# Softplus of delta for the other images in layer 0: three parts summed by TensorE, the positive part added by VectorE

## The chip, the cores and the metric

One NeuronCore of a Trainium2 chip runs the whole four-layer program as one launch. The time is the device time of one execution in microseconds (us); the number compared is the median of several executions. The other seven cores do nothing.

## The reference

Four layers act on an activation of 4 images x 64 x 64 tokens x 128 channels. Only layer 0, a selective scan (Mamba style) over 256 inner channels and 16 states, is touched. What matters of it:

```
xz = x @ w_in;  xc, z = split(xz)
xa = silu(depthwise_conv3x3(xc) + conv_b)              # 256 channels, 4096 tokens
dts, B, C = split(xa @ w_xproj, [8, 24])
delta = softplus(dts @ w_dt + b_dt)                    # 256 x 4096 for every image
# four directions (rows, columns, and both reversed) share delta, B and C:
h = h * exp(delta_i * A) + (delta_i * u_i) * B_i       # 16 states a channel, 4096 steps
y_i = sum_n h * C_i
```

The kernel computes softplus(x) as max(x, 0) + ln(1 + u) plus a small correction, with u = exp(-|x|): with w = 1 + u as rounded, the correction is u - (w - 1), that is, what the rounding of w lost.

## The kernel before

Layer 0 works image by image. For an image and a half h of the channels (128 of 256) there are 64 chunks of 64 tokens; the main loop runs over I, that is over 4 images x 2 halves x 64 chunks = 512 iterations. An iteration does, for the four directions in two pairs (kp = 0 and 1):

- `products(now, kp)` (L850): 16 small matmuls on TensorE that write delta*u*B of two directions into two PSUM buffers `db`. There are three such buffers.
- `scan(...)`: on VectorE, two adds of the carry into the first column (L865) and two scans of 1024 columns (L870), from `db` and the decay `dA` into the SBUF tile `big`; then on GpSimd the carry `cy` of the next chunk (L877) and the product of `big` with C (L885), 128 x 2048.
- `inputs(nxt)` (L826), VectorE, in the first half only: delta*u of the next iteration.
- `total(I - 2, part)` (L905): 8 matmuls on TensorE that sum the states of the iteration two back into the one PSUM tile `yp`; after part 1, ScalarE copies `yp` out in four pieces (L919). Part 0 of the next iteration writes `yp` again.
- `decay(w, ...)` (L773): on ScalarE, four exponentials for the next group of four chunks.

Beside this, a generator `beside` does the preparation of the next image in small steps. It is advanced once in the first half of an iteration (after `total(I - 2, 0)`, before the decays and `products(now, 1)`) and once in the second half (after `total(I - 2, 1)` and the four copies). All of its steps share one PSUM bank, `bg`. Images 1 to 3 go through `front` (norm and input projection) and then, from chunk 0 of the second channel half of the image before, through `middle`: eight blocks of 512 tokens, each of 14 steps, so seven iterations a block. Of a block's steps, numbered 0 to 13: 0 to 3 convolve and transpose, 4 projects, 5 turns B, 6 to 9 make delta for the two channel halves, 10 to 13 transpose and flip delta and store it. Even steps fall into first halves and odd ones into second halves. Image 0 is prepared before the loop by another function (`opening`), which the change leaves alone.

Steps 6 and 8 of before hold, for one half of the channels each, the matmul with `w_dt` (L426) and five ScalarE activations (L491 to L496): |x|, max(x, 0), u, w = 1 + u written into the bank, and ln w. Steps 7 and 9 hold the three VectorE operations L498, L501 and L502, which read and write the bank, and the store of delta (`keep_steps`, L432).

The loop stands under `tc.manual_schedule` for TensorE, ScalarE and VectorE: these three issue in exactly the order in which the program is written. GpSimd's and the DMA queue's (SP) order is the scheduler's. The SBUF tiles of the preparation come from a ring of ten buffers, `t2k`.

Of the kernel before, what the change touches and what calls it, by code (L numbers as in the profile page):

```python
# [8 lines left out]
AF = mybir.ActivationFunctionType  # L9
ALU = mybir.AluOpType  # L10
# [4 lines left out]
P = 128  # L15
# [5 lines left out]
BLK = 512  # L21
# [39 lines left out]
def tl(pool, shape, tag, dtype=F32, bufs=None):  # L61
    return pool.tile(shape, dtype, name=tag, tag=tag, bufs=bufs)
# [99 lines left out]
def layer0(cm, x, W, x1, also, ahead, kept):  # L162


    tc, nc = cm.tc, cm.nc
    wl = kept.enter_context(tc.tile_pool(name="l0k", bufs=1))
    dr = kept.enter_context(tc.tile_pool(name="l0dram", bufs=2, space=DRAM))
    with ExitStack() as ctx:
        ctx.enter_context(nc.allow_non_contiguous_dma(reason="parameters laid over partitions"))
        wp = ctx.enter_context(tc.tile_pool(name="l0w", bufs=1))  # L170
        tmp = ctx.enter_context(tc.tile_pool(name="l0t", bufs=10))
# [66 lines left out]
        for i in range(2):  # L238
            t = tl(wp, [P, QC, 2, NH0, TC], f"dA{i}")
# [16 lines left out]
        for i in range(2):  # L256
            t = tl(wp, [P, 8, PADW], f"padded{i}")
# [108 lines left out]
        def shifted(i, pool, tag, queue=nc.sync):  # L366

            k, h = divmod(i, 2)
            x3 = [tl(pool, [3 * CG, 2, 8 * PADW], tag) for _ in range(2)]
            for dy in range(3):  # L370
                s0 = (8 * k + dy) * PADW
                for i in range(2):
                    queue.dma_start(
                        x3[i][dy * CG : (dy + 1) * CG],
                        xc_d[4 * h + 2 * i : 4 * h + 2 * i + 2, :, s0 : s0 + 8 * PADW]
                        .rearrange("g p s -> p g s"),
                    )
            return x3

        def convolved(ps, h, x3):  # L380
            for dx in range(3):
                for g in range(4):
                    nc.tensor.matmul(  # L383
                        ps[g * CG : (g + 1) * CG, :], lhsT=cdiag[:, 4 * h + g, dx, :],
                        rhs=x3[g // 2][:, g % 2, :].rearrange(
                            "p (r w) -> p r w", w=PADW
                        )[:, :, dx : dx + HW],
                        start=(dx == 0), stop=(dx == 2),
                    )

        def columns(ps, src):
            for i in range(4):
                nc.tensor.transpose(
                    ps[:, i * P : (i + 1) * P], src[:, i * P : (i + 1) * P], cm.ident
                )

        def keep_turned(b, h, k, t):
            nc.sync.dma_start(
                img[b]["xT"][h, k * BLK : (k + 1) * BLK, :].rearrange("(t p) c -> p t c", p=P), t
            )  # L400

        def projected(ps, xa):
            for h in range(2):
                nc.tensor.matmul(
                    ps[0:NX, :], lhsT=w_xp[:, h, :], rhs=xa[h], start=(h == 0), stop=(h == 1)
                )

        def keep_c(b, k, xd):
            nc.sync.dma_start(
                img[b]["ct"][8 * k : 8 * k + 8].rearrange("c n t -> n c t"),  # L410
                xd[RANK + NST : NX, :].rearrange("n (c t) -> n c t", t=TC),
            )

        def turned_b(ps, k, xd, xr):
            pb = ps[:, 0 : 8 * NST].rearrange("p (c n) -> p c n", n=NST)
            for c in range(8):
                for j in range(2):
                    nc.tensor.matmul(
                        pb[j * TC : (j + 1) * TC, c, :],
                        lhsT=xr[0:NX, c, :] if j else xd[0:NX, c * TC : (c + 1) * TC],  # L420
                        rhs=cm.ident[0:NX, RANK : RANK + NST], start=True, stop=True,
                    )
            nc.vector.tensor_copy(BT[:, 8 * k : 8 * k + 8, :], pb)

        def steps(ps, h, xd):
            nc.tensor.matmul(  # L426
                ps, lhsT=w_dt[:, h * P : (h + 1) * P], rhs=xd[0:RANK, :],
                start=True, stop=True,
            )

        def keep_steps(b, h, k, r):
            nc.sync.dma_start(img[b]["dl"][h, :, k * BLK : (k + 1) * BLK], r)  # L432

        def flipped(ps, t):
            nc.tensor.matmul(
                ps, lhsT=flip, rhs=t.rearrange("p t c -> p (t c)"), start=True, stop=True
            )

        def keep_both(b, h, k, j, t):
            for i in range(2):  # L440
                nc.sync.dma_start(
                    img[b]["dT"][h, 8 * k + i : 8 * k + 8 : 2, j]
                    .rearrange("t r c -> r t c"), t[i * TC : (i + 1) * TC],
                )

        def middle(b, bank, pool, tag, ahead):

            ready = [shifted(i, pool, tag) for i in range(ahead)]
            for k in range(NBLK):
                cols = slice(k * BLK, (k + 1) * BLK)  # L450
                xa = []
                for h in range(2):
                    ps = bank()
                    convolved(ps, h, ready.pop(0))
                    if 2 * k + h + ahead < 2 * NBLK:
                        ready.append(shifted(2 * k + h + ahead, pool, tag))
                    xh = tl(tmp, [P, BLK], "t2k")
                    nc.scalar.activation(xh, ps, AF.Silu, bias=vec[:, 0, h : h + 1])
                    y0 = tl(tmp, [P, BLK], "t2k")
                    nc.scalar.activation(y0, xh, AF.Copy, scale=d4[:, h : h + 1])  # L460
                    nc.sync.dma_start(img[b]["y0"][:, h, cols], y0)
                    xa.append(xh)
                    yield
                    ps = bank()
                    columns(ps, xa[h])
                    t = tl(tmp, [P, 4, P], "t2k")
                    nc.scalar.copy(t, ps.rearrange("p (t c) -> p t c", c=P))
                    keep_turned(b, h, k, t)
                    yield
                ps = bank()  # L470
                projected(ps, xa)
                xd = tl(tmp, [P, BLK], "t2k")
                nc.scalar.copy(xd[0:NX, :], ps[0:NX, :])
                xr = tl(tmp, [P, 8, TC], "t2k")
                nc.scalar.copy(
                    xr[0:NX], ps[0:NX, :].rearrange("p (c t) -> p c t", t=TC)[:, :, ::-1]
                )
                keep_c(b, k, xd)
                yield
                turned_b(bank(), k, xd, xr)  # L480
                rs = []
                for h in range(2):
                    yield


                    ps = bank()
                    steps(ps, h, xd)
                    bias = vec[:, 1, h : h + 1]
                    u = tl(tmp, [P, BLK], "t2k")
                    r = tl(tmp, [P, BLK], "t2k")  # L490
                    nc.scalar.activation(u, ps, AF.Abs, bias=bias)  # L491
                    nc.scalar.activation(r, ps, AF.Relu, bias=bias)
                    nc.scalar.activation(u, u, AF.Exp, scale=-1.0)
                    nc.scalar.activation(ps, u, AF.Identity, bias=cm.ones[:, 0:1])
                    v = tl(tmp, [P, BLK], "t2k")
                    nc.scalar.activation(v, ps, AF.Ln)  # L496
                    yield
                    nc.vector.scalar_tensor_tensor(  # L498
                        ps, ps, 1.0, u, ALU.subtract, ALU.subtract
                    )  # L500
                    nc.vector.tensor_tensor(ps, v, ps, ALU.subtract)  # L501
                    nc.vector.tensor_tensor(r, ps, r, ALU.add)  # L502
                    keep_steps(b, h, k, r)
                    rs.append(r)

                yield
                for h in range(2):
                    t = None
                    for j in range(2):
                        ps = bank()  # L510
                        if j == 0:
                            columns(ps, rs[h])
                        else:
                            flipped(ps, t)
                        t = tl(tmp, [P, 4, P], "t2k")
                        nc.scalar.copy(t, ps.rearrange("p (t c) -> p t c", c=P))
                        keep_both(b, h, k, j, t)
                        yield
# [215 lines left out]
        def place(I):  # L734
            u, c = divmod(I, NCHUNK)
            return divmod(u, 2) + (c,)
# [237 lines left out]
        with tc.manual_schedule(engines=engines):  # L974
            for I in range(N):
                b, h, c = place(I)
# [19 lines left out]
                w = quads.get(I // QC + 1)  # L996
# [1829 lines left out]
```

## Time and profile before

| | |
|---|---|
| median of 3 executions | 10080.76 us (10066.63 to 10089.57) |
| the profiled execution | 10065.04 us, its span 10063.1 us |
| busy in the span | TensorE 8590.0, VectorE 7471.3, GpSimd 5373.5, ScalarE 5347.1 us |
| the chain that ended last | TensorE 42%, VectorE 26%, GpSimd 10% |
| the scans of layer 0 | from 219.5 us to 5653 us of the span |

The profile lists groups of equal instructions: line, engine, operation, output<-input with shapes and count, then total busy time in us and the mean of one in ns, then the idle time of that engine just before them and what ended most of it. The timeline lists instructions by start, with the duration; a bracket gives the idle time before and what ended it. Where equal instructions follow each other, the duration runs from the first start to the last end. A matmul's duration includes the way through the array, so the distance to the next start says more of the rate; a matmul of this type (f32) leaves two records. The table of stretches gives each engine's busy time and count in a stretch of the span, and the TensorE clock that was granted (1.00 is full speed).

### The profile page before, as it was taken

The page shows a single profiled execution, that of the slowest core. Times are in us where ns is not written, and L with a number is a line of the kernel's source. Part 1 is how long each engine was busy: PE and PEld are TensorE (multiplying, and loading weights), DVE is VectorE, ACT ScalarE, POOL GpSimd, SP SyncE. Part 2 cuts the span into 40 slices and gives each one's busy share as a digit, 9 for nine tenths or more (in the row PEclk, how much of TensorE's full clock was granted, in tenths as well). Part 3 has the DMA queues.
Part 4 walks back from the last instruction along what each step waited for, and adds up shares of the span by engine and source line. Part 5 has one row for each costly group of instructions (what it writes and reads, how often), then busy time and mean ns, then how long its engine had stood idle before and what let it go on. Part 6 is the DMA issues. An engine that isn't in the chain of part 4 may idle for free.

```text
span 10063.1 us, 193320 instructions
## 1 busy us (share of the span) xinstructions
PE 8590.0 (85%) x73048; PEld 4219.2 (42%) x73048; DVE 7471.3 (74%) x11089; ACT 5347.1 (53%) x13309; POOL 5373.5 (53%) x2788
## 2 busy tenths in 40 slices
PE   7888888889988899988888649999999958888776
PEld 3333444444434444444333334444444435554442
DVE  4999999999999999999999765454551123455656
ACT  5775555775547665556522237767776613443331
POOL 4999999899999899999999500000000000100000
PEclk8899999999999999999999869999999977888887
DMA  7344454445543455444333321111101062212101
GB/s 212 103 132 128 137 141 114 128 130 146 145 126 120 120 160 144 132 120 124 87 103 94 107 66 31 37 38 34 38 18 33 16 223 48 61 45 52 43 24 47
DMA packets 1081627, 957.38 MB, mean 95 GB/s; under 512 B 165356, under 2 KB 825616, under 8 KB 1073920
## 3 DMA queue, kind: packets, MB, share of 16 engines
q1 hardware_dynamic: 1055298, 880.82, 29.7%
q0 software_dynamic: 18560, 63.37, 3.4%
q8 instruction: 586, 9.60, 0.4%
q14 instruction: 337, 2.76, 0.1%
q10 hardware_dynamic: 6846, 0.83, 0.1%
HBM read 608.77 MB, written 335.80 MB: 94 GB/s over the span
## 4 chain that ended last, share of the span: by engine, by line
PE 42%; DVE 26%; POOL 10%; issue 8%; ACT 6%; DMA 5%; SPq 2%; DVEq 0%; ACTq 0%; POOLq 0%
DVE big L870 15%; POOL big L885 8%; PE qk L1758 7%; PE av L1817 7%; PE yp L905 5%; PE db L850 4%; PE x L2607 2%; DVE tex L2613 2%; DVE du L826 2%; PE s L2373 1%; DMA xo<-xT_d 1%; PE po L2398 1%; PE bg L383 1%; DVE mx L2337 1%; PE s L2331 1%
## 5 line engine op out<-in xcount | busy, mean ns | idle before, releaser
L885 POOL TENSOR_TENSOR big<-big,ct 128x2048 f32<-128x2048 f32 x1024 | 4659.0, 4550 | 76.1
L870 DVE TENSOR_TENSOR_SCAN big<-dA,db 128x1024 f32<-128x1024 f32 x2048 | 4571.0, 2273 | 13.6 <-DMA xo<-xT_d 8.6
L850 PE MATMUL db<-dg,du 32*64 32x256 f32 x32768 | 1896.0, 418 | 606.0 <-DVE big L870 466.6
L905 PE MATMUL yp<-big,both 128*64 128x256 f32 x16384 | 2229.3, 419 | 60.5 <-ACT yc L919 47.6
L905 PEld LDWEIGHTS yp<-big,both 128*64 128x64 f32 x16384 | 1191.8, 148 | 1031.0 <-issue 563.6
L850 PEld LDWEIGHTS db<-dg,du 32*64 32x64 f32 x32768 | 653.3, 135 | 1791.9 <-issue 1692.3
L1817 PE MATMUL av<-e,x 128*128 128x512 f32 x2048 | 974.0, 592 | 4.6 <-ACT e L1812 4.6
L1762 ACT ACTIVATE e<-qk,nk 128x512 f32<-128x512 f32 x1024 | 692.6, 685 | 534.1 <-PE qk L1758 533.2
L1758 PE MATMUL qk<-a,xT 128*128 128x512 f32 x2048 | 966.6, 594 | 8.6 <-ACT e L1762 7.9
L919 ACT COPY yr<-yp 128x64 f32<-128x64 f32 x1024 | 221.7, 216 | 1346.9 <-PE yp L905 1331.4
L818 ACT ACTIVATE dg<-mask,BT 128x32 f32<-128x32 f32 x4096 | 896.6, 318 | 10.9 <-PE db L850 8.6
L773 ACT ACTIVATE dA<-dp,A 128x252 f32<-128x252 f32 x2048 | 866.0, 498 | 49.8 <-issue 26.1
L1331 POOL TENSOR_TENSOR g_rs<-g_rs,k_qrow 128x4 f32<-128x4 f32 x32 | 41.0, 1282 | 1499.9 <-DVE g_rs L1330 1499.9
L1758 PEld LDWEIGHTS qk<-a,xT 128*128 128x128 f32 x2048 | 378.0, 190 | 462.3 <-issue 358.0
L1817 PEld LDWEIGHTS av<-e,x 128*128 128x128 f32 x2048 | 381.6, 190 | 434.7 <-issue 393.2
L1812 ACT ACTIVATE e<-e 128x1024 f32<-128x1024 f32 x510 | 538.7, 1056 | 15.4
L877 POOL TENSOR_TENSOR cy<-big,a 128x32 f32<-128x32 f32 x1008 | 365.6, 363 | 299.6 <-DVE big L870 239.3
L2380 ACT ACTIVATE e<-s 128x576 f32<-128x576 f32 x448 | 272.7, 647 | 398.8 <-PE s L2373 396.2
L2112 POOL TENSOR_TENSOR ln_rs<-ln_rs,mroot 128x4 f32<-128x4 f32 x64 | 64.8, 1012 | 756.0 <-DVE ln_rs L2111 501.6
L2392 POOL COPY vp<-vt 112x80 f32<-112x80 f32 x112 | 30.2, 270 | 781.2 <-PE po L2398 755.3
L2613 DVE SCALAR_TENSOR_TENSOR tex<-x,gw,tex 128x128 f32<-128x128 f32 x768 | 264.5, 344 | 198.0 <-PE x L2607 184.3
L826 DVE TENSOR_TENSOR du<-xo,dt 128x256 f32<-128x256 f32 x512 | 387.7, 757 | 0.0
(569 smaller groups left out, 9805.6 us busy)
## 6 DMA issues: line engine op xcount, KB each, us to landing
ct<-ct_d SPq DMA_DIRECT2D x1024, 128.0 KB
xo<-xT_d SPq DMA_DIRECT2D x2048, 32.0 KB
dg_d<-dg SPq DMA_DIRECT2D x256, 256.0 KB
dg<-dg_d SPq DMA_DIRECT2D x256, 256.0 KB
t4k<-xc_d SPq DMA_DIRECT2D x288, 132.0 KB
dp<-dl_d SPq DMA_DIRECT2D x256, 128.0 KB
dT_d<-t2k SPq DMA_DIRECT2D x256, 128.0 KB
dt<-dT_d SPq DMA_DIRECT2D x512, 64.0 KB
```

What stands on the lines that cost most here:

```text
L773: nc.scalar.activation(w["dA"][:, :, g, n, 1:], w["dp"][:, g, :, 1:], AF.Exp, scale=A[:, w["h"], g, n : n + 1],)
L818: nc.scalar.activation(q["dg"][:, n, :], mask, AF.Copy, scale=BT[:, q["c"], n : n + 1])
L826: nc.vector.tensor_tensor(q["du"], q["xo"], q["dt"].unsqueeze(1).to_broadcast([P, 2, P]), ALU.mult)
L850: nc.tensor.matmul(bs[j][p * TC : (p + 1) * TC, g * NH0 : (g + 1) * NH0, t0 : t0 + QR], lhsT=q["du"][rows, kp, g * TC : (g + 1) * TC], rhs ...
L870: nc.vector.tensor_tensor_scan(st[:, u].rearrange("p n t -> p (n t)"), q["w"]["dA"][:, c % QC].rearrange("p g n t -> p (g n t)"), bs[j].re ...
L885: nc.gpsimd.tensor_tensor(sv, sv, q["ct"].rearrange("p n t -> p (n t)").unsqueeze(1) .to_broadcast([P, 4, NH0 * TC]), ALU.mult,)
L905: nc.tensor.matmul(yp[p * TC : (p + 1) * TC], lhsT=both, rhs=st[:, :, p * NH0 + n, :], start=(n == 0), stop=(n == NH0 - 1),)
L1758: nc.tensor.matmul(ps, lhsT=me["xT"][:, kt * P : (kt + 1) * P], rhs=me["a"][k], start=True, stop=True,)
L1762: nc.scalar.activation(e[:, j, :], ps, AF.Exp, bias=me["nk"][:, kt : kt + 1], scale=2.0)
L1812: nc.scalar.activation(es[g + 2], es[g + 2], AF.Exp)
L1817: nc.tensor.matmul(avs[b, k], lhsT=img[b]["x"][:, kt, :], rhs=e[:, j, :], start=(kt == 0), stop=(kt == NT - 1),)
L2613: nc.vector.scalar_tensor_tensor(t[:, i, :], s[:, e * D : (e + 1) * D], gw[:, j, 4 * a + e : 4 * a + e + 1], t[:, i, :], ALU.mult, ALU.add,)
```

## The change

For both halves h, the ScalarE parts are now made first, in steps 6 and 7. w goes into an SBUF tile instead of the bank, and after ln w a sixth activation replaces w by 1 - w. Steps 8 and 9 then sum ln w, 1 - w and u by three matmuls with the identity into the bank, and one VectorE addition adds max(x, 0). The number of steps of a block stays 14. A block takes 20 tiles from the ring instead of 18.

```diff
                 turned_b(bank(), k, xd, xr)
+                parts = []
+                for h in range(2):
+                    yield
+                    ps = bank()
+                    steps(ps, h, xd)
+                    bias = vec[:, 1, h : h + 1]
+                    u, r, w, v = [tl(tmp, [P, BLK], "t2k") for _ in range(4)]
+                    nc.scalar.activation(u, ps, AF.Abs, bias=bias)
+                    nc.scalar.activation(r, ps, AF.Relu, bias=bias)
+                    nc.scalar.activation(u, u, AF.Exp, scale=-1.0)
+                    nc.scalar.activation(w, u, AF.Identity, bias=cm.ones[:, 0:1])
+                    nc.scalar.activation(v, w, AF.Ln)
+                    nc.scalar.activation(w, w, AF.Identity, scale=-1.0, bias=cm.ones[:, 0:1])
+                    parts.append([v, w, u, r])
                 rs = []
                 for h in range(2):
                     yield
                     ps = bank()
-                    steps(ps, h, xd)
-                    bias = vec[:, 1, h : h + 1]
-                    u = tl(tmp, [P, BLK], "t2k")
-                    r = tl(tmp, [P, BLK], "t2k")
-                    nc.scalar.activation(u, ps, AF.Abs, bias=bias)
-                    nc.scalar.activation(r, ps, AF.Relu, bias=bias)
-                    nc.scalar.activation(u, u, AF.Exp, scale=-1.0)
-                    nc.scalar.activation(ps, u, AF.Identity, bias=cm.ones[:, 0:1])
-                    v = tl(tmp, [P, BLK], "t2k")
-                    nc.scalar.activation(v, ps, AF.Ln)
-                    yield
-                    nc.vector.scalar_tensor_tensor(
-                        ps, ps, 1.0, u, ALU.subtract, ALU.subtract
-                    )
-                    nc.vector.tensor_tensor(ps, v, ps, ALU.subtract)
+                    r = parts[h].pop()
+                    for i, t in enumerate(parts[h]):
+                        nc.tensor.matmul(
+                            ps, lhsT=cm.ident, rhs=t, start=(i == 0), stop=(i == 2)
+                        )
                     nc.vector.tensor_tensor(r, ps, r, ALU.add)
                     keep_steps(b, h, k, r)
                     rs.append(r)
```

More of the change, by code (lines that the diff above doesn't have):

```diff
@@ L480, in middle @@
                 turned_b(bank(), k, xd, xr)
-                rs = []
+                parts = []
                 for h in range(2):
@@ L493, in middle @@
                     nc.scalar.activation(u, u, AF.Exp, scale=-1.0)
-                    nc.scalar.activation(ps, u, AF.Identity, bias=cm.ones[:, 0:1])
-                    v = tl(tmp, [P, BLK], "t2k")
-                    nc.scalar.activation(v, ps, AF.Ln)
-                    yield
-                    nc.vector.scalar_tensor_tensor(
-                        ps, ps, 1.0, u, ALU.subtract, ALU.subtract
-                    )
-                    nc.vector.tensor_tensor(ps, v, ps, ALU.subtract)
+                    nc.scalar.activation(w, u, AF.Identity, bias=cm.ones[:, 0:1])
+                    nc.scalar.activation(v, w, AF.Ln)
+                    nc.scalar.activation(w, w, AF.Identity, scale=-1.0, bias=cm.ones[:, 0:1])
+                    parts.append([v, w, u, r])
+                rs = []
+                for h in range(2):
+                    yield
+                    ps = bank()
[4 more added lines that the diff above has]
+                        )
                     nc.vector.tensor_tensor(r, ps, r, ALU.add)
```

## Prediction

> **What bounds the kernel now.** I read the page's costliest groups first.
>
> ```profile
> L885 POOL TENSOR_TENSOR big<-big,ct 128x2048 f32<-128x2048 f32 x1024 | 4659.0, 4550 | 76.1
> L870 DVE TENSOR_TENSOR_SCAN big<-dA,db 128x1024 f32<-128x1024 f32 x2048 | 4571.0, 2273 | 13.6 <-DMA xo<-xT_d 8.6
> ```
>
> The scans of layer 0 run without a gap for 5433 of the span's 10063 us: VectorE stood idle before them for 13.6 us in all. GpSimd is as full. An iteration in which VectorE has no preparation work takes 9.83 us (scans start at 1041.16 and 1050.99). So whatever VectorE does beside the scans lengthens the stage. What it does for softplus is in the groups by shape:
>
> ```profile
> L501 DVE TENSOR_TENSOR bg<-t2k,bg 128x512 f32<-128x512 f32 x48 | 33.4, 696 | 1.6
> L494 ACT ACTIVATE bg<-t2k,ones 128x512 f32<-128x512 f32 x48 | 33.2, 692 | 1.6
> L502 DVE TENSOR_TENSOR t2k<-bg,t2k 128x512 f32<-128x512 f32 x48 | 33.2, 691 | 1.6
> L498 DVE SCALAR_TENSOR_TENSOR bg<-bg,t2k 128x512 f32<-128x512 f32 x48 | 32.4, 674 | 0.0
> ```
>
> Three operations, 48 times each (24 blocks, two halves). Then the timeline of TensorE around steps 6 to 9 of one block (image 1, block 1), and around a convolution:
>
> ```profile
> 1008.70 1.12 PE L426 MATMUL bg<-t2k,w_dt 8*128 8x512 f32 x2
> 1009.75 1.91 PE L850 MATMUL db<-dg,du 32*64 32x256 f32 x32
> 1011.59 1.95 PE L905 MATMUL yp<-big,both 128*64 128x256 f32 x16
> 1013.47 0.66 PE L850 MATMUL db<-dg,du 32*64 32x256 f32 x8
> 1015.28 1.45 PE L850 MATMUL db<-dg,du 32*64 32x256 f32 x24 [1.15 <-DVE big L870]
> 1018.05 3.48 PE L905 MATMUL yp<-big,both 128*64 128x256 f32 x16 [1.32 <-ACT yc L919]
> ...
> 1050.23 1.95 PE L905 MATMUL yp<-big,both 128*64 128x256 f32 x16
> 1052.11 2.78 PE L383 MATMUL bg<-t4k,cdiag 96*32 96x512 f32 x24
> 1054.82 0.69 PE L850 MATMUL db<-dg,du 32*64 32x256 f32 x16
> 1055.66 0.69 PE L850 MATMUL db<-dg,du 32*64 32x256 f32 x16 [0.15 <-issue]
> 1056.28 1.95 PE L905 MATMUL yp<-big,both 128*64 128x256 f32 x16
> ```
>
> Two things show. TensorE waited 1.32 us for ScalarE's copies of yp, and then its total took 3.48 instead of 1.95 us. ScalarE's rows say why the copies came late, and the table of stretches why the total was slow:
>
> ```profile
> 1009.86 0.69 ACT L491 ACTIVATE t2k<-bg,vec 128x512 f32<-128x512 f32 x1 [5.20 <-PE bg L426]
> ...
> 1014.29 1.28 ACT L807 ACT_TABLE_LOAD   x1
> ...
> 1017.63 0.28 ACT L919 COPY yc<-yp 128x64 f32<-128x64 f32 x1
> ```
>
> ```profile
> 1014.40:1017.80 3.40, 1.35 (x24) 0.48 (x24) 3.40 (x3) 3.39 (x10) 3.32 (x3) 1.00 0.41 110
> 1017.80:1021.20 3.40, 3.15 (x16) 1.90 (x16) 3.33 (x6) 0.11 (x1) 3.40 (x1) 0.50 0.19 49
> ```
>
> Columns: stretch, length, then busy us of TensorE, its weight loads, VectorE, ScalarE, GpSimd, then the clock. In a stretch of 3.4 us TensorE was busy for 1.35 us, and in the next its clock was halved.
>
> **The change, part by part.** Times are in us after 1000 in this block; n is the iteration whose scan starts at 7.77, the next three start at 19.48, 31.09 and 41.16.
>
> Removed: L498 and L501, start to start 0.70 + 0.73 = 1.43 a half, 2.86 a block, 69 us over 24 blocks. VectorE was the bound, so all of it would come off the time if nothing else took its place; L502 stays (0.69).
>
> Added to ScalarE: one activation a half, start to start 0.71 as L494 (11.67 to 12.38). w going to SBUF instead of PSUM changes nothing that I can price: L493, SBUF to SBUF, takes 0.63, L494 0.69; I leave it at 0, with 0.06 to either side. Steps 6 and 7 put both halves' activations into one iteration. ScalarE had 4.4 us idle before the second half's, so it has room; but the copies of yp stand behind step 6's activations and the decays, and they come 0.7 later.
>
> Added to TensorE: three matmuls of 512 columns a half, 144 in all. The nearest row is the convolution: 24 records in four column groups at once, that is three f32 matmuls one after another, 2.71 from start to next start. Lower end: no cheaper row exists, so 2.7. Upper end: three times the lone flip matmul (38.07 to 39.13), 3.2. I take 2.7, since these too run back to back.
>
> The chain, at full clock:
> - Step 6: as before; TensorE is free at 13.47. Step 7: the second half's w_dt matmul goes first, 1.05, to 14.52; the products then still wait for a db buffer until 15.28, as before, and end at 16.73. So this matmul costs 0, hidden in the 1.15 wait; uncovered it would be 1.05. VectorE has no work in step 7: the scan of n+1 starts at 17.23 + 0.25 = 17.48 instead of 19.48, a gain of 2.0.
> - The copies end at 17.91 + 0.71 = 18.62, so total(n-1, 0) starts at 18.75 instead of 18.05. Queued behind it on TensorE: its own 1.88 (to 20.63), the first sum 2.71 (23.34; the parts are long done), the products 1.46 (54.82 to 56.28) to 24.80. The scan starts 0.39 after (56.28 to 56.67): 25.19. VectorE was ready earlier: scans to 21.86, delta*u 0.4 to 0.75, the add once the sum is there (23.4 to 24.1). It loses 1.1 before the add and 0.8 before the carry adds. The scan stood at 24.39 before: now 0.8 late.
> - Second half of n+1: total 1.88, second sum 2.71, products 1.46, all behind each other: 24.80 to 30.85; scan of n+2 at 31.24. VectorE would be ready at 30.5. The second half's parts: ScalarE starts them at 18.6 after the copies, 5.1 long, to 23.7, in time for 26.7. Before: 31.09.
> - n+2: total 1.88, the transposes 0.6, products 1.46 to 34.8; VectorE 31.24 + 4.38 + 0.40 + 0.25 = 36.27, now the later one; n+3 at 36.27 + 4.58 = 40.85, before 41.16.
>
> So at full clock a block gains 0.3, not 2.86: relief of VectorE turns into waiting for TensorE, which holds 6.05 a half against VectorE's 4.6 to 5.4.
>
> The clock is the other term. Before, the three iterations took 33.39 here; over the 24 blocks, read from the scans' starts, 32.8 to 36.8, mean 34.17. The long ones have half clock for four stretches:
>
> ```profile
> 2424.10:2427.50 3.40, 2.25 (x26) 1.18 (x12) 3.33 (x7) 1.46 (x7) 3.32 (x3) 0.50 0.31 72
> ```
>
> is the first of four (to 2437.70); ten blocks are of this kind. After, TensorE idles once, from 16.73 to 18.75. Cut into stretches of 3.4 us, layer 0 shows at full clock: of 63 with TensorE busy for under 0.5 of it, 62 were followed by half clock, of 86 between 0.5 and 0.6, 71, of 120 between 0.6 and 0.7, 38. A gap of 2.0 brings some stretch under 0.6 in about 85 of 100 positions. A stretch of half clock takes 1.7 of work from a chain on the path, 1.6 allowing for what falls into the gap: +1.35 a block. In about one of ten positions the first half-clock stretch is itself thin and the state should last four stretches: total 3.6, sum 5.4, products 2.4, total and rest, together +6: +0.6 a block. Expected: 33.08 + 1.95 = 35.0 against 34.17, +0.85 x 24 = +20 us.
>
> [...] The rows above show gaps of 1.15 and 1.32 in one stretch ending in half clock, so I go by them.
>
> Small edits. The first half's store of delta (L432) moves one step later; in SP's queue it now stands ahead of one xo load, dg and ct of a coming iteration, which therefore wait for the add until 24.1; they are used from 35 on, and landing takes a few us, so 0. The second half's store keeps its step. Twenty tiles of a ring of ten: each new tile's predecessor was last read four or more steps (over 20 us) earlier, or by an operation before it on the same chain: 0. ScalarE's table loads keep their number (L496 and the return to exp, once a half). GpSimd gets nothing; it idles 1.4 and 1.8 in these halves before and will again.
>
> **Rivals.**
> - *No half clock.* The step-7 matmul fills what was the first gap, and the remaining gap falls across two stretches. Then 33.1 a block, -1.1 x 24 = -26 us. Against it: gaps of 1.3 to 2.4 were followed by half clock in most blocks.
> - *VectorE's relief passes through* (faster): if the sums hide in TensorE's slack, -2.86 x 24 = -69, near 10012. It decides where the first sum ends before delta*u does (22.3 to 22.6); the chain puts it at 23.34 at the earliest. For it: before, TensorE waited 466.6 us for scans over the kernel, so slack exists elsewhere.
> - *Long half clock* (slower): if the state lasts four stretches in as many blocks as before (10 of 24), 33.1 + 0.58 x 1.6 + 0.42 x 6 = 36.5, +2.4 x 24 = +57; with sums of 3.2 (two a block, +1.0) +81. For it: those blocks exist. Against it: TensorE is busy without a break from 18.75 on.
>
> **How the numbers follow.** The profiled execution took 10065.04 (span 10063.1 and 1.9 around it), 16 below the median of 10080.76; differences are carried to the median: 10080.76 + 20 = 10101. Its own range, with one half-clock stretch in none to two of the blocks more or less and 2.7 to 3.2 for a sum: 0 to +45. About 0.2% (20 us) is what a measurement of this kernel can tell from no change. Main case 0.62, half of it above +20. Long half clock 0.17, slower. No half clock 0.12, of which 0.07 faster and 0.05 same. VectorE's relief 0.09, faster. Faster 0.16, same 0.36, slower 0.48. The range, -36 to +74, reaches into the no-drop and long cases and leaves out about 0.16, mostly the 10012.
>
> **What would show it.** L498 and L501 gone, 288 records of matmuls with ident into bg. VectorE waits before the remaining add for those matmuls, about 1 us in 24 of 48, and before L865 for the products, about 0.7 in all 48: some 60 us of new idle time. ScalarE's wait for L426 (251.8 us) falls by about half. The scan distances n, n+1, n+2 read 9.7, 13.8, 9.6 at full clock, 15.4 in the middle one with one stretch of half clock. Wrong would be: iterations of 10.4 and 10.4 (VectorE-bound), a total that does not wait for the copies, or sums under 2 us.

## The result and the profile after

The changed kernel takes 10097.28 us (median of 17 runs, 10082.81 to 10111.26) against 10065.62 us of the kernel before (17 runs): ratio 1.0027, 95% interval 1.0021 to 1.0034, slower by about 27 us. The forecast of 10101 rested on the three earlier runs of the kernel before, 15 us above its later median; so the effect was +27 (by the ratio) to +32 us (by the medians) where +20 was forecast. That the total came closer than the effect did is luck.

The profiled execution's span grew from 10063.1 to 10095.4 us. First scan to last scan it grew by 29.8 us (5431.6 to 5461.4). Per block, from scan start to scan start (n is again the iteration in which step 6 falls):

| mean of 24 blocks, us | n | n+1 | n+2 | together |
|---|---|---|---|---|
| before | 12.04 | 12.31 | 9.82 | 34.17 |
| after | 10.21 | 15.15 | 9.69 | 35.04 |
| forecast, full clock | 9.7 | 13.8 | 9.6 | 33.1 |
| forecast, with half clock | | | | 35.0 |

0.87 x 24 = 21 of the 29.8 us lie in these iterations. The other 9 are spread over the rest of the stage and were not traced to a cause. The first scan starts 7.9 us later in this execution and the layers behind take 5.4 less; in the profiles of the other kernels below the first scan starts anywhere from 221 to 227 us, so it is not put down to the change.

Groups by shape; the first line is of the kernel before, the others of the kernel after (the last column is the idle time before, and what ended it):

```profile
L865 DVE TENSOR_TENSOR db<-db,cy 128x16 f32<-128x16 f32 x2016 | 254.7, 171 | 72.2 <-PE db L850 68.2 <-POOL a L763 2.5
L503 PE MATMUL bg<-t2k,ident 128*128 128x512 f32 x288 | 139.0, 619 | 0.0
L506 DVE TENSOR_TENSOR t2k<-bg,t2k 128x512 f32<-128x512 f32 x48 | 33.1, 690 | 48.9 <-issue 29.9 <-PE bg L503 19.0
L869 DVE TENSOR_TENSOR db<-db,cy 128x16 f32<-128x16 f32 x2016 | 256.3, 171 | 101.9 <-PE db L854 97.3 <-DVE db L869 1.4 <-POOL a L767 1.3
```

VectorE's remaining addition now has 48.9 us of idle time before it, where it had 1.6, and the carry adds (L865, now L869) 101.9 where they had 72.2: 77 us of new waiting. Against it stand the 65.8 us that L498 and L501 were busy (68.6 from start to start). Part of that is lost elsewhere: delta*u took 395.8 us in all instead of 387.7; why is not shown. The timeline of TensorE in the same block as before (n starts at 1015.63):

```profile
1021.32 1.12 PE L426 MATMUL bg<-t2k,w_dt 8*128 8x512 f32 x2
1022.37 2.21 PE L854 MATMUL db<-dg,du 32*64 32x256 f32 x32
1026.73 3.29 PE L909 MATMUL yp<-big,both 128*64 128x256 f32 x16 [2.15 <-ACT yc L923]
1029.95 2.84 PE L503 MATMUL bg<-t2k,ident 128*128 128x512 f32 x6
1032.72 0.69 PE L854 MATMUL db<-dg,du 32*64 32x256 f32 x16
1034.18 1.95 PE L909 MATMUL yp<-big,both 128*64 128x256 f32 x16
```

The gap before the total (2.15), the slow total (3.29 instead of 1.95), the sum (2.77 to the next start) and the products follow each other as forecast. The last of the copies that the total waits for ends 10.95 us after n's start:

```profile
1026.30 0.28 ACT L923 COPY yc<-yp 128x64 f32<-128x64 f32 x1
```

VectorE in the same half:

```profile
1029.65 0.77 DVE L830 TENSOR_TENSOR du<-xo,dt 128x256 f32<-128x256 f32 x1
1032.89 0.69 DVE L506 TENSOR_TENSOR t2k<-bg,t2k 128x512 f32<-128x512 f32 x1 [2.47 <-issue]
1034.36 0.29 DVE L869 TENSOR_TENSOR db<-db,cy 128x16 f32<-128x16 f32 x2 [0.78 <-PE db L854]
```

It stands for 2.47 us until the sum is there (the sum's last record ends at 1032.79; the page books this as "issue") and for 0.78 more for the products. The stretches (length, busy us of TensorE, weight loads, VectorE, ScalarE, GpSimd, then the clock):

```profile
1022.70:1026.10 3.40, 1.68 (x32) 0.48 (x24) 3.40 (x5) 3.37 (x9) 3.32 (x3) 1.00 0.29 88
1026.10:1029.50 3.40, 2.77 (x14) 1.82 (x16) 3.40 (x2) 3.35 (x9) 3.40 (x1) 0.50 0.24 66
```

### The profile page after: what moved, and what is told of

The parts are those of the page before. It is cut to its first block, busy times and chain, and to the rows that moved or that the text cites. A ratio compares the mean times of both kernels' runs of the same rounds, so it can differ in the third digit from the quotient of the medians.

```text
span 10095.4 us, 193915 instructions
## 1 busy us (share of the span) xinstructions
PE 8664.9 (86%) x73336; PEld 4251.4 (42%) x73336; DVE 7420.6 (74%) x10993; ACT 5384.3 (53%) x13357; POOL 5375.3 (53%) x2788
## 3 DMA queue, kind: packets, MB, share of 16 engines
q14 instruction: 337, 2.76, 0.1%
## 4 chain that ended last, share of the span: by engine, by line
PE 46%; DVE 24%; issue 8%; POOL 7%; ACT 6%; DMA 6%; SPq 2%; DVEq 0%; ACTq 0%; POOLq 0%
DVE big L874 13%; PE qk L1762 7%; PE av L1821 7%; PE yp L909 7%; POOL big L889 6%; PE db L854 5%; PE x L2611 2%; DVE tex L2617 2%; DVE du L830 1%; PE bg L383 1%; PE s L2377 1%; PE bg L503 1%; DMA xo<-xT_d 1%; PE po L2402 1%; PE mm L2296 1%
## 5 line engine op out<-in xcount | busy, mean ns | idle before, releaser
L854 PE MATMUL db<-dg,du 32*64 32x256 f32 x32768 | 1872.4, 413 | 568.6 <-DVE big L874 431.1
L822 ACT ACTIVATE dg<-mask,BT 128x32 f32<-128x32 f32 x4096 | 896.6, 318 | 12.2 <-PE db L854 9.9
L1816 ACT ACTIVATE e<-e 128x1024 f32<-128x1024 f32 x510 | 538.7, 1056 | 15.4
L2396 POOL COPY vp<-vt 112x80 f32<-112x80 f32 x112 | 29.8, 266 | 774.0 <-PE po L2402 748.2
L830 DVE TENSOR_TENSOR du<-xo,dt 128x256 f32<-128x256 f32 x512 | 395.8, 773 | 0.0
```

The lines of the kernel that those rows point to most:

```text
L822: nc.scalar.activation(q["dg"][:, n, :], mask, AF.Copy, scale=BT[:, q["c"], n : n + 1])
L830: nc.vector.tensor_tensor(q["du"], q["xo"], q["dt"].unsqueeze(1).to_broadcast([P, 2, P]), ALU.mult)
L854: nc.tensor.matmul(bs[j][p * TC : (p + 1) * TC, g * NH0 : (g + 1) * NH0, t0 : t0 + QR], lhsT=q["du"][rows, kp, g * TC : (g + 1) * TC], rhs ...
L1816: nc.scalar.activation(es[g + 2], es[g + 2], AF.Exp)
```

## Experiments

The theory: VectorE's relief is lost because in n+1 everything waits for one chain, ScalarE's late copies of yp, then total, sum and products on TensorE; and after the gap before the total TensorE runs at half clock (1.00 and then 0.50 in the two stretches above). The rivals: the added matmuls alone cost (added work); or the clock alone does. "Changed" is the kernel after; every ratio is to the kernel before, run beside it on the same chip. The experiments ran on three chips, so they are compared by these ratios and not by their times. In the edits, `begun / first / decay` stands for the three calls that make the decays, and `...` for lines left out.

**1. Decays after step 7 (the copies come early), first version.**

```diff
-                if w: begun / first / decay            # before products(now, 1)
+                late = h and b + 1 < B and c < 56 and c % 7 in (3,) and c % QC < QC - 1
+                if not late: begun / first / decay
...
+                if late: begun / first / decay          # after the second half's step
```

> The changed kernel, but in the iteration of step 6 (18 of 24 blocks; not where a group of four chunks ends) the four decays stand after step 7 in ScalarE's order, so the copies of yp no longer wait for them. Held-chain theory (TensorE waits for late copies, goes to half clock, and its chain total - sum - products then sets the scans): the copies end 3 us sooner, the 2.0 us gap goes and with it the half clock; n+1 falls from 15.2 to about 12 us, the three iterations from 35.0 to about 31.3 us, so -3.7 x 18 = -65 us, near 10030, below the kernel before. Added-work theory (the sums' 5.4 us a block are what costs, gap and clock are incidental): the sums are all there still, so within 10 us of the changed kernel. Clock-only theory: -1.6 x 18 = -29 us.

10068.45 us, ratio 1.0001 (0.9992 to 1.0010). The expectation was met in a quarter of the places only: the condition on the chunk holds for image 1, while the blocks of images 2 and 3 stand four chunks later. In the six blocks it met, n+1 fell from 14.9-15.7 to 11.8-12.2 us, and no half clock began from step 7 up to the sums. The copies now end 7.81 us after n's start, which is at 1008.22 here, instead of 10.95:

```profile
1015.74 0.29 ACT L923 COPY yc<-yp 128x64 f32<-128x64 f32 x1
1014.96 2.21 PE L854 MATMUL db<-dg,du 32*64 32x256 f32 x32
1017.10 1.95 PE L909 MATMUL yp<-big,both 128*64 128x256 f32 x16
1018.98 2.84 PE L503 MATMUL bg<-t2k,ident 128*128 128x512 f32 x6
```

TensorE (experiment 1, the same block) goes from the products to the total without a gap. The sums are as long as before (2.84 us).

**2. The same in the kernel before** (chunks of steps 6 and 8).

```diff
+                late = h and b + 1 < B and c < 56 and c % 7 in (3, 4) and c % QC < QC - 1
```

> The kernel before with the same move of the decays, in the iterations of steps 6 and 8. Held-chain theory: its waits for the copies (1.3 and 2.4 us) and their half-clock stretches go in most blocks, but VectorE's three operations still set the pace: three iterations 34.2 to about 32.7 us in 18 blocks, -25 us, near 10040. The gain is less than half of that of the changed kernel, since TensorE was not the later one there. Added-work theory: nothing to gain, within 10 us of the kernel before.

10064.47 us, ratio 0.9994 (0.9985 to 1.0003). No gain; it too met image 1 only, where the late copies were hidden behind VectorE's three operations (n+1 11.5 to 11.8 with and without). By itself this is also what the added-work theory expected; experiment 3 decides between the two.

**3. Second version, at the right chunks.**

```diff
-                late = h and b + 1 < B and c < 56 and c % 7 in (3,) and c % QC < QC - 1
+                late = h and b + 1 < B and 2 < c < 58 and (c - (4 if b else 0)) % 7 in (3,) and c % QC < QC - 1
```

> The first version of this move met step 6 only in image 1, since the blocks of images 2 and 3 stand four chunks later; now it meets it in 18 of 24 blocks. Where it met it, n+1 fell from 14.9-15.7 to 11.8-12.2 us without half clock. Held-chain theory: the same in the other images, -3.4 x 18 = -61 us against the changed kernel, near 10036, below the kernel before. Added-work theory: no more than the first version, near 10068.

10031.16 us, ratio 0.9974 (0.9963 to 0.9985). As expected: the 18 blocks it meets take 32.06 us for the three iterations, the six it leaves out 35.04. In two of the 18 (chunk 42) it did not help (35.67 and 35.48 us): there the products had waited 1.8 us for a `db` buffer, and half clock followed although the copies were early. With the copies early in the others, the change is a gain; the added matmuls, all still there, are hidden.

**4. The same in the kernel before.**

```diff
+                late = h and b + 1 < B and 2 < c < 58 and (c - (4 if b else 0)) % 7 in (3, 4) and c % QC < QC - 1
```

> The kernel before with the same move at the right chunks, in steps 6 and 8. In image 1 the first version changed nothing (n 11.7, n+1 11.6 us): there VectorE's three operations set the pace and the late copies were hidden. What is left to gain are the blocks with half clock for four stretches (n+1 13.4 us): held-chain theory -1.9 x 9 = -17 us, near 10050. So the late copies should cost the kernel before at most a third of what they cost the changed one (61 us). If the copies cost both kernels alike: -61 us.

10060.92 us, ratio 1.0004 (0.9995 to 1.0013). The expected 17 us did not come: n+1 fell from 12.31 to 11.76, but n+2 rose from 9.82 to 10.57, since stretches of half clock now fall 14 to 28 us after n's start. So the move gains the kernel before nothing, and the changed kernel some 50 us (1.0027 to 0.9974).

**5. TensorE kept busy in step 7, 8 rows.**

```diff
-                    steps(ps, h, xd)
+                    for _ in range(3 if h else 1):
+                        steps(ps, h, xd)
```

> The changed kernel with the w_dt matmul of the second half run three times in step 7 instead of once (the same result, 2.1 us more of TensorE work a block). Held-chain theory: the repeats fill the gap before the late copies, which shrinks from 2.0 to about 0.6 us; no half clock follows; the chain starts at the same moment and runs at full speed: -1.6 x 24 = -38 us, near 10060. Added-work theory: 2.1 x 24 = +50 us, near 10147. If the gap matters but not the clock: no change.

10105.11 us, ratio 1.0030 (1.0018 to 1.0042). No gain, and no 50 us of loss. The repeats took 1.7 us a block (three w_dt matmuls 2.76, one 1.05); n went from 10.21 to 11.12, and most of that came back in n+1 (15.15 to 14.43). The time is that of the third branch ("no change"), but the run does not test it, since the half clock stayed, in all 24 blocks. In the block shown the wait for the copies shrank to 1.03 us, and the half clock began after a stretch that by the records was nearly full (3.25 of 3.40 us):

```profile
1028.26 3.68 PE L910 MATMUL yp<-big,both 128*64 128x256 f32 x16 [1.03 <-ACT yc L924]
```

```profile
1023.50:1026.90 3.40, 3.25 (x38) 1.10 (x36) 3.19 (x2) 3.34 (x7) 3.40 (x2) 1.00 0.38 114
1026.90:1030.30 3.40, 2.37 (x23) 1.40 (x12) 3.02 (x4) 3.37 (x10) 3.32 (x2) 0.51 0.21 52
```

**6. The same with 128 rows.**

```diff
+                    for _ in range(2 * h):
+                        nc.tensor.matmul(ps, lhsT=cm.ident, rhs=w_in, start=True, stop=True)
                     steps(ps, h, xd)
```

> The first filler used the w_dt matmul, of 8 rows; the half-clock stretch then began right after 3.4 us in which TensorE's records are gapless, so 8-row matmuls may not hold the clock. Now the filler in step 7 is two matmuls of 128 rows (identity times w_in, into the bank, before the w_dt matmul overwrites it). If rows matter and the clock is a term of its own: no half-clock stretch in most blocks, n+1 near 13.1 us, n 10.3, three iterations 33.1 instead of 35.0 us, -1.9 x 24 = -45 us, near 10055. If the added work is what costs: +2.1 x 24 = +50 us. If the gap before the copies costs and the clock does not: as the first filler, near 10105.

10071.95 us, ratio 1.0007 (0.9997 to 1.0017): work that does nothing makes the changed kernel faster by about 20 us, half of the 45 expected. In 14 of 24 blocks no half-clock stretch fell near the chain any more, and there n+1 takes 12.94 us on average; in the ten others 14.67, with n the same in both (10.8). So the clock is a term of 1.7 us a block by itself. Timeline and stretch of a block without it:

```profile
1020.05 1.95 PE L911 MATMUL yp<-big,both 128*64 128x256 f32 x16 [0.92 <-ACT yc L925]
```

```profile
1017.17:1020.58 3.41, 2.34 (x40) 0.94 (x40) 2.65 (x4) 3.40 (x12) 3.33 (x3) 1.00 0.28 80
```

The total still waits for the copies (0.92 us), and then takes 1.95 us and not 3.29, in a stretch at clock 1.00. n and n+1 are typically 10.5 + 13.0 = 23.5 us in such a block, what the forecast's chain has at full clock (9.7 + 13.8).

**7. One matmul instead of three** (1 - w and u are left out of the sum).

```diff
-                    for i, t in enumerate(parts[h]):
-                        nc.tensor.matmul(ps, lhsT=cm.ident, rhs=t, start=(i == 0), stop=(i == 2))
+                    nc.tensor.matmul(ps, lhsT=cm.ident, rhs=parts[h][0], start=True, stop=True)
```

> The changed kernel with one matmul instead of three in steps 8 and 9 (only ln w is brought to the bank; 1 - w and u are left out of the sum, which drops a correction of the size of a rounding). It sizes the sums. Held-chain theory: the first half of n+1 starts its scan about 1.7 us sooner, the second is then VectorE-bound, -2.6 us a block, -63 us, near 10035. Added-work theory, all of it on the path: -3.4 x 24 = -82 us, near 10015. If the late copies and the clock alone cost: -10 us or less.

10029.12 us, ratio 0.9960 (0.9946 to 0.9973). As the theory had it: n+1 12.74, three iterations 32.66, -2.4 a block where -2.6 was expected, and -3.4 by the added-work theory. The half clock is still there in all 24 blocks. The sums are on the path only because they stand behind the late copies; experiments 3 and 7 take one of the two away each and gain nearly the same.

**8. The halves apart again** (parts, sum, parts, sum in steps 6 to 9; the sums stay).

```diff
-                parts = []
+                rs = []
...
-                    parts.append([v, w, u, r])
-                rs = []
-                for h in range(2):
                     yield
                     ps = bank()
-                    r = parts[h].pop()
-                    for i, t in enumerate(parts[h]):
+                    for i, t in enumerate((v, w, u)):
```

> The changed kernel without its second part: the halves stand apart again (parts in step 6, sum in 7, parts in 8, sum in 9). Held-chain theory: in step 7 the sum waits 1.5 us for its parts (ScalarE ends them 5.1 us after the w_dt matmul), so the first scan of n+1 comes as late as before (n 11.7 us); the copies' wait is then covered by the sum, and the second half's parts hold the sum of step 9 by about 1.8 us, n+1 12.5 to 14 us, n+2 9.7. Three iterations 34 to 35.4 us: within 25 us of the changed kernel, to the fast side if anything. If having both halves' parts first is what made the change slow (ScalarE's queue of twelve activations): three iterations under 33 us, -50 us or more.

10042.41 us, ratio 0.9977 (0.9968 to 0.9986). My expectation was wrong, and its second branch right: three iterations take 32.97 us, 2.1 less than in the changed kernel. TensorE shows why:

```profile
1013.01 2.84 PE L497 MATMUL bg<-t2k,ident 128*128 128x512 f32 x6 [0.85 <-ACT t2k L492]
...
1017.49 1.95 PE L903 MATMUL yp<-big,both 128*64 128x256 f32 x16 [0.18 <-ACT yc L917]
...
1025.07 2.84 PE L497 MATMUL bg<-t2k,ident 128*128 128x512 f32 x6 [1.24 <-ACT t2k L492]
```

The first sum starts as soon as ln w is there, before 1 - w, so it waits 0.85 and not 1.5 us; it then fills the time until the copies, and the total waits 0.18 us. The copies themselves come as late as in the changed kernel (they end 10.96 us after n's start). Nearly no half clock is left (one stretch in 24 blocks, before a chain). So the summation by TensorE is a gain by itself, and "both halves' parts first" is what turned it into a loss: it leaves step 7 without TensorE work that would cover the late copies, and puts the first sum behind them.

**9. The six blocks left out in 3, too** (there the decays stand between the copies and step 7).

```diff
+                if late and c % QC == QC - 1: begun / first / decay    # before the second half's step
                 next(beside, None)
+                if late and c % QC < QC - 1: begun / first / decay
```

> As the second move of the decays, and in the six blocks left out there (where a group of four chunks ends) the decays stand between the copies of yp and step 7, since the next iteration needs them. Held-chain theory: in these blocks the copies end about 3 us sooner, the next scan waits about 1 us for the decays, the gap before the total and the half clock go: three iterations from 35.0 to about 33.3 us, -1.7 x 6 = -10 us against the second move, near 10022.

10032.75 us, ratio 0.9961 (0.9947 to 0.9974). The six blocks fell from 35.04 to 33.14 us on average, as expected; in the whole time it can't be told from experiment 3.

**10. A version without sums** (no correction for the rounding of w; both halves first). The edit is shown against the changed kernel; the three matmuls of the sum go too.

```diff
-                    nc.scalar.activation(w, u, AF.Identity, bias=cm.ones[:, 0:1])
-                    nc.scalar.activation(v, w, AF.Ln)
-                    nc.scalar.activation(w, w, AF.Identity, scale=-1.0, bias=cm.ones[:, 0:1])
+                    nc.scalar.activation(v, u, AF.Ln, bias=cm.ones[:, 0:1])
...
+                    nc.vector.tensor_tensor(rs[h], vs[h], rs[h], ALU.add)
```

> Both halves' parts first, but no sums on TensorE: four activations a half (ln taken with its bias of one, so neither w nor 1 - w is made), and one VectorE addition of two SBUF tiles in steps 8 and 9. It leaves out the correction for the rounding of w. Held-chain theory: with neither the sums nor the late copies (ScalarE's chain to the copies is 1.5 us shorter), n+1 is VectorE-bound, 11.1 to 11.4 us, no half clock: three iterations 30.5 to 30.9 us, -3.4 x 24 = -82 us against the kernel before, near 9980. If the relief of VectorE is handed to GpSimd (9.8 us an iteration is its floor, and the SBUF addition is held up while it works): 32 us and more, -50 us or less.

10014.93 us, ratio 0.9949 (0.9935 to 0.9962), the lowest of all, but a gain of some 51 us and not 82. n+1 is 11.38 us as expected, but the three iterations take 31.59 and not 30.5 to 30.9: n+2 rose to 10.21. In number that is nearer to the expectation's second branch, but GpSimd is not what holds n+2: it is 10.2 to 10.7 us in the 12 blocks with two stretches of half clock from about 18 to 20 us after n's start on, and 9.5 to 9.7 in ten of the other 12. TensorE, relieved, waits 2.00 us for a buffer, and the total that follows takes 3.68 us instead of 1.95:

```profile
1027.66 2.25 PE L843 MATMUL db<-dg,du 32*64 32x256 f32 x24 [2.00 <-DVE big L863]
1029.85 3.68 PE L898 MATMUL yp<-big,both 128*64 128x256 f32 x16
```

## Why the prediction was right

- *VectorE's relief turns into waiting.* Right, and shown: 65.8 us of VectorE's work gone (69 forecast, from start to start), 77 us of new idle time before the addition and the carry adds. The estimate of the waits, some 60 us, was low because it took the wait before the first addition at full clock, 1.1 us; at half clock it is 2.47 in the block shown. Experiment 6 has both: 2.0 to 2.3 us in most blocks with half clock, at most 0.63 in those without.
- *The chain starts with the late copies.* Right: shown by experiments 1, 3 and 9, which move nothing but the decays, so that the copies come sooner, and take the loss away in most blocks they meet (16 of 18 in experiment 3), and by 2 and 4, in which the same move gains nothing where VectorE sets the pace.
- *The chain's terms.* The sum was 2.77 (2.71 forecast, from the convolution's row), the total and the products as their rows; the sixth activation 0.73 to the next start (0.71). The scan starts of n+1 and n+2 lie where the chain has them with one stretch of half clock (9.64 and 15.48 us in the block shown, 9.7 and 15.4 forecast).
- *Step 7's matmul is hidden.* Right: n is 9.6 to 10.3 in most blocks. ScalarE's wait for L426 fell from 251.8 to 130.1 us, by about half as forecast.
- *The clock.* The size was right (1.6 forecast, 1.7 in experiment 6), the count was not: I expected one stretch in about 85 of 100 blocks and four stretches in about 10; all 24 have one near 8 to 13 us after n's start, in three blocks it lasts two stretches, and none lasts four. The sum of the two, +1.95 a block, came out as it should (35.0 forecast, 35.04 measured) with the terms off in opposite directions, which is luck. (Of the ten long blocks counted before, nine have four stretches of half clock and one has three.)
- *What was off:* the effect, +20 against some +27 to +32. 9 us of it lie outside the three iterations and stay open.
- The rival "no half clock" is what experiment 6 makes of it in 14 blocks. "VectorE's relief passes through" is what experiment 3 comes near to once the copies come early, at 32.06 us in the blocks met (34.17 - 2.86 = 31.3 would be all of it; the best have 31.05). Its condition, the first sum ending before delta*u, was the right one: in the block of the timelines above the sum ends 13.6 us after n's start in experiment 3, delta*u 14.8.

## What to carry over

Taking work off the busiest engine pays only where the next engine in line has its inputs early; here that was decided by four small copies that stood behind six activations and the decays in ScalarE's program order; the added work cost time only because it queued behind them. Before moving steps of a pipeline together, see what each of them covers: the step that was left empty had hidden a wait. A cheap reordering of the queue that feeds the chain turned 27 us lost into 26 gained; on the kernel before the same reordering gained nothing, so each paid only with the other.

## Not expected of the hardware

TensorE's clock was halved after a stretch of 3.4 us in which its records show 3.25 us busy (experiment 5, all of it in matmuls of 8 and 32 rows; 1.00 there, 0.51 in the next stretch), and not after one with 2.34 us busy, of which matmuls of 128 rows were 0.53 us (experiment 6, both blocks shown above). Experiment 6 has the same contrast within one kernel; in the first of these two stretches TensorE is busy for 3.06 us, and in the second it has a clock of 0.50:

```profile
2730.66:2734.07 3.41, 3.06 (x35) 0.97 (x34) 3.41 (x2) 3.40 (x11) 3.41 (x1) 1.00 0.44 118
2734.07:2737.49 3.42, 3.23 (x16) 1.90 (x16) 3.42 (x5) 3.37 (x6) 3.34 (x3) 0.50 0.33 96
```

Over the 24 blocks of experiment 6, of the full-clock stretches that end 7 to 14.5 us after n's start, TensorE's busy share is 0.69 to 0.90 in the ten followed by half clock and 0.69 to 1.00 in the 42 others. So up to 0.90 the busy share, by which the forecast counted its stretches, does not tell these apart; what halves the clock was not shown. The two fillers, of about the same length, differ by 0.23% of the time, some 23 us (ratios 1.0030 and 1.0007), with half clock near the chain in all 24 blocks of experiment 5 and in ten of experiment 6.
